# PSUM as four pairs of banks, and the second tiles' masks after their scores, in a planned fp32 transformer kernel

## The chip, the core and the metric

The kernel runs on one NeuronCore of a Trainium2 chip. The metric is device time in microseconds (us) of one execution, the median of several. The engines are called by the names of the profile: PE (matmuls; PEld is its weight load), ACT, DVE and POOL (elementwise work), SP (which issues the DMAs).

## What is computed

The input is 32 sequences of 256 tokens and 128 channels. Each goes through half a feed-forward block, an attention over channels, and half a feed-forward block again, always with a residual; the two blocks use the same weights. A feed-forward block (`_L0_ffn_ref`) has two layers, and each layer is a local attention followed by a gated MLP:

```
qkv = shift_token(x) @ wqkv              # 8 heads of 64
q, k = l2norm(q) * qs, l2norm(k) * ksc   # then rotary
sim = q . k over a window                # key j of query i: i-64 <= j <= i
x = x + (softmax(sim) @ v) @ wo
h = layernorm(shift_token(x)) @ w1 + b1  # 128 -> 2 x 341
x = x + (a * gelu(g)) @ w2 + b2
```

So there are 32 x 2 x 2 = 128 layers to compute, each in two tiles of 128 tokens. All data is fp32.

## The kernel before

**A plan in place of loops.** The Python code first makes a list of operations (`plan.op`), each with its engine, a cost in us, the operations that it follows, and the places that it uses: SBUF and PSUM buffers, taken by kind with `plan.take`. `Plan.order` then sets the order of all engines. It goes through the list in stretches of 15 PE operations, tries 16 orders for the next 60 PE operations with its own costs, keeps the one in which PE ends first, and commits the stretch. `Plan.go` takes the operation that can start first by `begin`, gives it its buffers (the free buffer of its kind that came free first) and moves the clock of its engine. `Plan.run` then writes the instructions in that order, with scheduling otherwise off. The waits between engines are put in afterwards by the framework, which looks at the tiles that instructions read and write.

**PSUM.** There are eight banks of 512 fp32 for each partition. Lines 112 and 113 make two "wide" tiles of two banks and four "bank" tiles of one bank, each a tile of its own. A wide tile holds the Q/K projection of a token tile (`project`, L197), the scores (`scores`, L247 and L255) and the attention output (`attended`, L289). A bank holds the V projection (L231), sets of transposes (`transposed`, L140), the output projection (L312), one third of the MLP's first product (L381), its second product (L414), and the products of the channel attention (L458). ACT empties most banks by copies (L130, `evac`; DVE in a few cases); DVE and ACT read the wide tiles (L203, L205, L208, L261, L264, L296, L297).

**Scores.** For each token tile, keys are cut into frames of 96 for blocks of 32 queries. Two bf16 matmuls of an identity with the mask (128x128 weights, 384 columns: four head pairs by 96) first write the mask into both banks, with start set; then 32 matmuls on 64x32 parts of the array add the scores. A value product is 32 matmuls of 96 rows by 32 columns (`attended`). An fp32 product is two matmul records in the profile, a transpose or a bf16 product one.

**Other buffers.** "gg" (three) holds the gelu half of the MLP between ACT (L389) and DVE (L396); "ob" (two) holds the divided attention output between DVE (L297) and its transposes. The prediction numbers lines as in the kernel before, except where it quotes the changed program.

Of the kernel before, what the change touches and what calls it, by code (L numbers as in the profile page):

```python
# [8 lines left out]
F32 = mybir.dt.float32  # L9
# [6 lines left out]
P = 128  # L16
# [24 lines left out]
def kernel(ctx: ExitStack, tc: tile.TileContext, ins: dict, out: bass.AP):  # L41
# [39 lines left out]
    for kind, n, shape in (  # L81
        ("x", CHAINS + 2, [P, NT, P]),
        ("y", CHAINS, [P, NT, P]),
        ("y3", CHAINS - 1, [P, NT, 3, P // 2]),
        ("xT", 2, [P, NT, P]),
        ("hT", SETS + 2, [P, SEQ]),
        ("qT", 4, [P, PAIRS, P]),
        ("kT", SETS, [P, PAIRS, SEQ]),
        ("vt", 2 * SETS + 1, [P, HEADS, DH + 1]),
        ("vm0", 3, [FR, 1, HEADS, DH + 1]),  # L90
        ("vm1", 2, [FR, 3, HEADS, DH + 1]),
        ("sq", 3, [P, 2, HEADS, DH]),
        ("qk", 4, [P, 2, HEADS, DH]),
        ("pr", 3, [P, 2, PAIRS, FR]),
        ("pT", 4, [P, PAIRS, P]),
        ("ob", 2, [P, INNER]),
        ("oT", 2, [P, PAIRS, P]),
        ("uT", 2, [P, len(HCH), SEQ]),
        ("z", 3, [P, NT, P]),
        ("zT", 2, [P, NT, P]),  # L100
        ("gg", 3, [P, SEQ]),
        ("cp", CHAINS + 1, [P, P]),
        ("ssq", 4, [P, 2, HEADS]),
        ("rn", 4, [P, 2, HEADS]),
        ("mx", 4, [P, 2, PAIRS]),
        ("rd", 4, [P, 2, PAIRS, 1]),
        ("st", 4, [P, NT, nc.vector.BN_STATS_DIM]),
        ("mv", 4, [P, NT, nc.vector.BN_AGGR_DIM]),
        ("v1", 12, [P, NT]),
    ):  # L110
        plan.places(kind, [hold.tile(shape, F32, name=f"{kind}{i}") for i in range(n)])
    for kind, n, shape in (("wide", 2, [P, 2, 512]), ("bank", 4, [P, 512])):
        plan.places(kind, [psum.tile(shape, F32, tag=f"{kind}{i}", name=f"ps_{kind}{i}", bufs=1) for i in range(n)])
    plan.places("sequence", range(CHAINS))

    for t in plan.free["vt"]:
# [122 lines left out]
    def scores(qT, kT, t, after):  # L239


        wide, mx, pr = (plan.take(k) for k in ("wide", "mx", "pr"))
        s = lambda: wide.t[:, :, : PAIRS * FR].rearrange("p r (j k) -> p r j k", k=FR)

        def mm(e):
            for r in range(2):
                nc.tensor.matmul(  # L247
                    s()[:, r], identh, masks[t].unsqueeze(1).to_broadcast([P, PAIRS, FR]), start=True, stop=False
                )
            for j in range(PAIRS):  # L250
                for b in range(NB):
                    k0 = frame(t, b)
                    for r in range(2):
                        row = slice(r * DH, (r + 1) * DH)
                        nc.tensor.matmul(  # L255
                            s()[b * BLK : (b + 1) * BLK, r, j, :], qT.t[row, j, b * BLK : (b + 1) * BLK],
                            kT.t[row, j, k0 : k0 + FR], start=False, stop=j == PAIRS - 1,
                        )

        m = plan.op("PE", 1.35, mm, after + [made["masks"][t]], [wide, qT, kT, mx, pr])  # L260
        a = plan.op("DVE", 0.87, lambda e: nc.vector.tensor_reduce(mx.t, s(), AX.X, ALU.max), [m], [wide, mx])  # L261
        b = plan.op(
            "DVE", 0.87,
            lambda e: nc.vector.tensor_sub(pr.t, s(), mx.t.unsqueeze(3).to_broadcast([P, 2, PAIRS, FR])),  # L264
            [a], [wide, mx, pr],
        )
        c = plan.op("ACT", 0.75, lambda e: nc.scalar.activation(pr.t, pr.t, AF.Exp), [b], [pr], table="exp")  # L267
        return pr, c

    def attended(pr, vt, vm, ob, t, after, values):  # L270

        mo, rd = plan.take("wide"), plan.take("rd")
        pTs, copies = [plan.take("pT") for r in range(2)], []
        for r in range(2):
            _, b = transposed(
                lambda r=r: [pr.t[:, r, j, :] for j in range(PAIRS)], PAIRS, lambda r=r: pTs[r].t[:FR], pTs[r],
                after, [pr, ob] + pTs, FR,
            )
            copies.append(b)
# [12 lines left out]

        m = plan.op("PE", 1.05, mm, copies + values, [mo, vt, vm, rd, ob] + pTs)

        def div(e):
            nc.vector.reciprocal(rd.t, o()[:, :, :, DH : DH + 1])  # L296
            nc.vector.tensor_mul(  # L297
                ob.t.rearrange("p (j r d) -> p r j d", r=2, d=DH), o()[:, :, :, 0:DH],
                rd.t.to_broadcast([P, 2, PAIRS, DH]),
            )  # L300

        return plan.op("DVE", 0.84, div, [m], [mo, rd, ob])
# [345 lines left out]
class Plan:  # L648
# [5 lines left out]

    SYNC = {"PE": 0.16, "DVE": 0.08, "ACT": 0.08, "POOL": 0.09, "SP": 0.08}
    TAIL = {"PE": 0.165, "ACT": 0.105, "DVE": 0.085, "POOL": 0.04, "SP": 0.0}
    RATHER = 1.0
    TABLE = 1.3
    TURNS = ("wide", "bank")
# [10 lines left out]
        pass  # L670

    def __init__(self):
        self.free, self.ops, self.rank, self.base = {}, [], 0, 0

    def places(self, kind, tiles):
        self.free[kind] = list(tiles)
# [1 line left out]
    def take(self, kind):  # L678
        return Plan.Place(kind)

    def op(self, engines, us, fn, after, uses, late=0.0, table=None, apart=False):
        o = Plan.Op()
        o.engines = (engines,) if isinstance(engines, str) else engines
        o.us = us if isinstance(us, tuple) else (us,)
        o.fn, o.late, o.table, o.apart = fn, late, table, apart
        o.rank, o.step = self.rank, len(self.ops) - self.base
        o.uses, o.then = [], []
        o.after = list(after)
        for d in o.after:
            d.then.append(o)  # L690
        self.ops.append(o)
        self.use(o, uses)
        return o
# [14 lines left out]
    def order(self, together):  # L708
# [2 lines left out]
        import random  # L711

        self.clock = dict.fromkeys(("PE", "DVE", "ACT", "POOL", "SP"), 0.0)
        self.table, self.through = None, 0
        self.room = {k: list(v) for k, v in self.free.items()}
        self.since = {k: [0.0] * len(v) for k, v in self.room.items()}
        for o in self.ops:
# [25 lines left out]

    def save(self):
        copy = lambda d: {k: list(v) for k, v in d.items()}
        return dict(self.clock), self.table, copy(self.room), copy(self.since), list(self.ready), len(self.out), self.through

    def back(self, saved):

        clock, self.table, room, since, ready, n, self.through = saved  # L750
        self.clock, self.ready = dict(clock), list(ready)
        self.room, self.since = ({k: list(v) for k, v in d.items()} for d in (room, since))
        for thing, state in reversed(self.undo):
            thing.__dict__.update(state)
        self.undo = []
        del self.out[n:]

    def lacks(self, o):
# [4 lines left out]
                need[p.kind] = need.get(p.kind, 0) + 1  # L763
        return need

    def begin(self, o, engine):

        t = max(o.given[engine], self.clock[engine], self.clock["POOL"] if o.apart else 0.0)
        sync = self.SYNC[engine]
        for p in o.uses:  # L770
            if p.last and p.last[1] != engine and p.kind in self.TURNS:
                t = max(t, p.last[0] + sync)
        for k, n in self.lacks(o).items():
            if len(self.room[k]) < n:
                return None
            t = max(t, (min(self.since[k]) if n == 1 else sorted(self.since[k])[n - 1]) + sync)
        return t

    def choose(self, o):

# [12 lines left out]
    def go(self, until, later, chance):  # L793
# [16 lines left out]
        while heap and (until is None or self.through < until):  # L810
            first, _, o = heapq.heappop(heap)
            choice = self.choose(o)
            if choice is None:
                barred.setdefault(next(k for k, n in self.lacks(o).items() if len(self.room[k]) < n), []).append(o)
                continue

            engine, t, us, rank = choice
# [4 lines left out]
            for p in o.uses:  # L822
                self.undo.append((p, dict(p.__dict__)))
                if p.t is None:
                    i = min(range(len(self.room[p.kind])), key=lambda i: self.since[p.kind][i])
                    p.t = self.room[p.kind].pop(i)
                    self.since[p.kind].pop(i)
                    taken.append((p, p.t))
                    for d in barred.pop(p.kind, []):
                        enter(d)  # L830
# [1 line left out]
            self.clock[engine] = t + us  # L832
            if o.apart:
                self.clock["POOL"] = t + us
            self.through += engine == "PE"
            self.undo.append((o, {"done": None}))
            o.done = (t + us + o.late + self.TAIL[engine], engine)
            if engine == "ACT" and o.table not in (None, self.table):
# [5 lines left out]
            for p in o.uses:  # L844
                p.left -= 1
                p.end, p.last = max(p.end, o.done[0]), o.done
                if not p.left:
                    self.room[p.kind].append(p.t)
                    self.since[p.kind].append(p.end)
                    for d in barred.pop(p.kind, []):  # L850
                        enter(d)
            for d in o.then:
                self.undo.append((d, {"wait": d.wait}))
# [57 lines left out]
```

## Time and profile before

| what | value |
|---|---|
| median of 3 runs | 2841.89 us (2840.95 to 2842.41) |
| the profiled execution | 2842.17 us |
| its span, first to last instruction | 2840.1 us |
| mean granted PE clock | 0.997 |
| busy: PE, DVE, ACT, POOL | 2788.2, 2135.1, 1993.7, 2302.2 us |
| DMA | 129.82 MB, mean 46 GB/s |

The page gives for each engine its busy time, then its busy share in 40 slices of the span (a digit is tenths). Groups of instructions are named by line, engine, output and inputs, with count and mean duration. A line of waits reads: who waited, for whom, us in total, how many times, the longest. A line of the timeline reads: start in us, length, engine, line, operation, output and inputs, rows by columns of the array, shape, count; a row merges equal neighbours, and since matmuls are pipelined its length overlaps the next start.

### The profile page before, as it was taken

How to read it: one execution, taken by the hardware profiler on the slowest of the kernel's cores; microseconds unless marked ns; L12 is line 12 of the kernel's file. 1: busy time of each engine (PE TensorE's matmuls, PEld its weight loads, DVE VectorE, ACT ScalarE, POOL GpSimd, SP SyncE). 2: the span in 40 equal slices, each digit the busy share in tenths (PEclk: the TensorE clock that was granted, in tenths of full speed). 3: DMA queues.
4: the chain of work that ended last, by engine and by line, in shares of the span. 5: the costliest groups of instructions: out<-in, count | busy, mean ns of one | idle time of the engine just before them, and what ended most of it. 6: DMA issues, size and time to landing. Idle time of an engine off the chain costs nothing.

```text
span 2840.1 us, 106723 instructions
## 1 busy us (share of the span) xinstructions
PE 2788.2 (98%) x46200; PEld 2114.4 (74%) x46200; DVE 2135.1 (75%) x3764; ACT 1993.7 (70%) x3601; POOL 2302.2 (81%) x2098
## 2 busy tenths in 40 slices
PE   7999999999999999999999999999999999999999
PEld 4777777777777777777777777777777777777677
DVE  5778778778777778677777777877787777777776
ACT  4776776767677776767777776776767677776675
POOL 8988879698889778787798878878788788875975
PEclk9999999999999999999999999999999999999999
DMA  3111121111211111111112112111121111110211
GB/s 109 31 46 44 38 52 47 39 51 37 55 38 47 46 40 48 38 49 45 44 51 53 46 36 52 46 36 47 47 55 47 37 46 44 43 46 20 53 42 41
DMA packets 125726, 129.82 MB, mean 46 GB/s; under 512 B 56606, under 2 KB 75592, under 8 KB 125256
## 3 DMA queue, kind: packets, MB, share of 16 engines
q1 hardware_dynamic: 124440, 122.60, 16.5%
q8 instruction: 363, 5.95, 0.9%
q14 instruction: 107, 0.88, 0.1%
q10 hardware_dynamic: 816, 0.39, 0.0%
HBM read 8.13 MB, written 4.19 MB: 4 GB/s over the span
## 4 chain that ended last, share of the span: by engine, by line
PE 86%; DVE 6%; ACT 3%; POOL 3%; issue 1%; DMA 1%; SPq 0%; ACTq 0%; DVEq 0%; POOLq 0%
PE ps_bank L140 20%; PE ps_wide L197 14%; PE ps_bank L381 11%; PE ps_wide L289 9%; PE ps_bank L312 8%; PE ps_wide L255 7%; PE ps_bank L231 7%; PE ps_bank L414 6%; PE ps_wide L247 3%; PE ps_bank L458 1%; PE ps_bank L178 1%; DVE qk L205 1%; DVE sq L208 1%; ACT sq L203 1%; POOL rn L124 1%
## 5 line engine op out<-in xcount | busy, mean ns | idle before, releaser
L124 POOL TENSOR_TENSOR rn<-ssq,mhalf 128x16 f32<-128x16 f32 x256 | 748.3, 2923 | 21.3
L222 POOL TENSOR_TENSOR qk<-qk,sq 128x1024 f32<-128x1024 f32 x256 | 606.4, 2370 | 163.8 <-DVE sq L208 83.4
L225 POOL TENSOR_TENSOR qk<-qk,rn 128x1024 f32<-128x1024 f32 x256 | 487.7, 1908 | 10.4
L197 PE MATMUL ps_wide<-wqkv,hT 128*128 128x512 f32 x1024 | 489.2, 600 | 2.0 <-ACT hT L130 1.2
L205 DVE TENSOR_TENSOR qk<-ps_wide,tab 128x1024 f32<-128x1024 f32 x256 | 312.2, 1219 | 184.7 <-ACT sq L203 101.7
L381 PE MATMUL ps_bank<-zT,w 128*128 128x256 f32 (+1 forms) x1536 | 379.3, 383 | 2.8 <-DVE zT L130 1.7
L203 ACT ACTIVATE sq<-ps_wide 128x1024 f32<-128x1024 f32 x256 | 262.5, 1025 | 154.2 <-PE ps_wide L197 91.6
L208 DVE TENSOR_TENSOR sq<-ps_wide,tab 128x1024 f32<-128x1024 f32 x256 | 311.4, 1217 | 66.8 <-ACT sq L203 32.6
L130 ACT COPY pT<-ps_bank 96x512 f32<-96x512 f32 x505 | 283.3, 584 | 101.1 <-PE ps_bank L140 98.7
L214 DVE TENSOR_REDUCE ssq<-sq 128x16 f32<-128x1024 f32 x256 | 310.0, 1211 | 57.2 <-ACT sq L203 56.4
L381 PEld LDWEIGHTS ps_bank<-zT,w 128*128 128x128 f32 (+1 forms) x1536 | 257.8, 178 | 70.8 <-issue 15.0
L140 PE MATMUL ps_bank<-ident,pr 128*96 128x128 f32 x2048 | 290.2, 275 | 5.1 <-ACT pr L267 2.4
L140 PE MATMUL ps_bank<-ident,qk 128*128 128x128 f32 x2048 | 290.8, 276 | 3.1 <-POOL qk L225 2.4
L261 DVE TENSOR_REDUCE mx<-ps_wide 128x8 f32<-128x768 f32 x256 | 242.9, 949 | 62.8 <-PE ps_wide L255 61.7
L197 PEld LDWEIGHTS ps_wide<-wqkv,hT 128*128 128x128 f32 x1024 | 179.4, 191 | 145.7 <-issue 133.3
L289 PE MATMUL ps_wide<-vt,pT 96*32 96x65 f32 x8192 | 282.1, 221 | 3.5 <-ACT pT L130 1.4
L289 PE MATMUL ps_wide<-vm,pT 96*32 96x65 f32 x8192 | 283.9, 221 | 1.5 <-DVE sq L208 0.7
L312 PE MATMUL ps_bank<-wo,oT 128*128 128x128 f32 x2048 | 275.9, 279 | 2.7 <-ACT oT L130 1.0
L140 PEld LDWEIGHTS ps_bank<-ident,qk 128*128 128x128 f32 x2048 | 236.4, 141 | 48.1 <-issue 24.0
L312 PEld LDWEIGHTS ps_bank<-wo,oT 128*128 128x128 f32 x2048 | 251.2, 191 | 27.1 <-issue 10.3
L140 PEld LDWEIGHTS ps_bank<-ident,pr 128*96 128x96 f32 x2048 | 225.1, 126 | 60.7 <-issue 29.3
L289 PEld LDWEIGHTS ps_wide<-vt,pT 96*32 96x32 f32 x8192 | 240.6, 109 | 37.8 <-issue 17.6
(101 smaller groups left out, 5430.1 us busy)
## 6 DMA issues: line engine op xcount, KB each, us to landing
vm<-vt SPq DMA_DIRECT2D x256, 195.0 KB
vm<-vt SPq DMA_DIRECT2D x256, 130.0 KB
vm<-vt SPq DMA_DIRECT2D x256, 65.0 KB
y<-y SPq DMA_DIRECT2D x128, 56.0 KB
x<-in_x SPq DMA_DIRECT2D x32, 128.0 KB
out<-x SPq DMA_DIRECT2D x32, 128.0 KB
y<-y SPq DMA_DIRECT2D x128, 7.5 KB
y<-y SPq DMA_DIRECT2D x128, 0.2 KB
```

The lines of the kernel that those rows point to most:

```text
L124: nc.gpsimd.tensor_tensor(dst, src, mhalf[:, :n], ALU.pow)
L140: nc.tensor.transpose(pt.t[:rows, j * P : (j + 1) * P], src, ident)
L197: nc.tensor.matmul(wide.t[:, a], lhsT(), wqkv[:, l, a * INNER : (a + 1) * INNER], start=True, stop=True)
L203: "ACT", 0.92, lambda e: nc.scalar.activation(sq.t, pq(), AF.Square), [m], [wide, sq]
L205: c = plan.op("DVE", 1.14, lambda e: nc.vector.tensor_mul(qk.t, pq(), cos), [m] + made["tables"][l], [wide, qk])
L208: lambda e: nc.vector.tensor_mul(sn.t.rearrange(five, x=2), pq().rearrange(five, x=2)[:, :, :, ::-1, :], sin.rearrange(five, x=2)),
L214: "DVE", 1.13, lambda e: nc.vector.tensor_reduce(ssq.t, sq.t, AX.X, ALU.add), [s], [sq, ssq]
L222: f = plan.op("POOL", 2.42, lambda e: nc.gpsimd.tensor_add(qk.t, qk.t, sn.t), [c, i], [qk, sn])
L225: lambda e: nc.gpsimd.tensor_mul(qk.t, qk.t, rn.t.unsqueeze(3).to_broadcast([P, 2, HEADS, DH])),
L289: nc.tensor.matmul(o()[q, r, j, :], pTs[r].t[:FR, j, q], v[:, 2 * j + r, :], start=True, stop=True)
L312: nc.tensor.matmul(pw.t[:, :P], oT.t[:, j, :], wo[:, l, j, :], start=j == 0, stop=j == PAIRS - 1)
L381: nc.tensor.matmul(pa.t[:w, i * SEQ : (i + 1) * SEQ], w1[:, l, i * HID + c0 : i * HID + c0 + w], zf(), start=True, stop=True,)
```

## The change

PSUM becomes four tiles of two banks each. A wide place takes a whole pair that is free in both banks; a bank place takes one bank, that is, a slice `[:, h, :]` of a pair's tile. Among the banks free in time it takes one of a pair whose other bank is not free, if there is one. What is given back may serve either kind.

For the second token tile of a layer (t = 1) the mask goes last: the first score matmul of each part has start set, and the mask is added after all scores. The mask is zero in the middle third of each frame of that tile, and only its first and last thirds are now loaded and added: 4 x 2 x 32 columns in place of 4 x 96. For the first tile all stays.

Each PE operation carries a form: how it finds and leaves the array (whole, parts, values). The plan keeps the form last left; a table of costs for changes of form stands beside it, which no line reads. The cost of the second tiles' scores in the plan goes from 1.35 to 1.16. There is one more place of "ob" and of "gg".

```diff
-        ("ob", 2, [P, INNER]),
+        ("ob", 3, [P, INNER]),
-        ("gg", 3, [P, SEQ]),
+        ("gg", 4, [P, SEQ]),
-    for kind, n, shape in (("wide", 2, [P, 2, 512]), ("bank", 4, [P, 512])):
-        plan.places(kind, [psum.tile(shape, F32, tag=f"{kind}{i}", name=f"ps_{kind}{i}", bufs=1) for i in range(n)])
+    plan.pairs = [psum.tile([P, 2, 512], F32, tag=f"pair{i}", name=f"ps_{i}", bufs=1) for i in range(4)]
+    plan.places("bank", [(i, h) for i in range(4) for h in range(2)])
...
         def mm(e):
-            for r in range(2):
-                nc.tensor.matmul(
-                    s()[:, r], identh, masks[t].unsqueeze(1).to_broadcast([P, PAIRS, FR]), start=True, stop=False
-                )
+            thirds = masks[t].rearrange("p (c k) -> p c k", k=BLK)[:, :: 1 + t, :]
+            def mask():
+                for r in range(2):
+                    nc.tensor.matmul(
+                        s()[:, r].rearrange("p j (c k) -> p j c k", k=BLK)[:, :, :: 1 + t, :], identh,
+                        thirds.unsqueeze(1).to_broadcast([P, PAIRS, thirds.shape[1], BLK]), start=t == 0, stop=t == 1,
+                    )
+            if t == 0:
+                mask()
...
-                            kT.t[row, j, k0 : k0 + FR], start=False, stop=j == PAIRS - 1,
+                            kT.t[row, j, k0 : k0 + FR], start=t == 1 and j == 0, stop=t == 0 and j == PAIRS - 1,
+            if t == 1:
+                mask()
-        m = plan.op("PE", 1.35, mm, after + [made["masks"][t]], [wide, qT, kT, mx, pr])
+        m = plan.op(
+            "PE", (1.35, 1.16)[t], mm, after + [made["masks"][t]], [wide, qT, kT, mx, pr],
+            form=(("all", "parts"), ("parts", "all"))[t],
+        )
...
+    CHANGE = {("all", "parts"): 0.09, ("all", "values"): 0.09, ("values", "values"): -0.11}
...
+    def whole(self):
+        since = {}
+        for (i, _), t in zip(self.room["bank"], self.since["bank"]):
+            since.setdefault(i, []).append(t)
+        return [(max(ts), i) for i, ts in since.items() if len(ts) == 2]
...
+    def grab(self, p, t):
+        room, since = self.room, self.since
+        if p.kind == "wide":
+            i = min(self.whole())[1]
...
+            p.t, p.bank = self.pairs[i], i
+            return
+        pick = lambda n: since[p.kind][n]
+        if p.kind == "bank":
+            here = [i for i, _ in room["bank"]]
+            pick = lambda n: (max(since["bank"][n] + self.SYNC["PE"], t), here.count(here[n]), since["bank"][n])
+        n = min(range(len(room[p.kind])), key=pick)
+        p.t = p.bank = room[p.kind].pop(n)
+        since[p.kind].pop(n)
+        if p.kind == "bank":
+            p.t = self.pairs[p.bank[0]][:, p.bank[1], :]
...
+    def give(self, p):
...
+        self.room["bank"] += [(p.bank, 0), (p.bank, 1)] if p.kind == "wide" else [p.bank]
+        self.since["bank"] += [p.end] * (2 if p.kind == "wide" else 1)
+        return "wide", "bank"
...
-            self.through += engine == "PE"
+            if engine == "PE":
+                self.through, self.array = self.through + 1, o.form[1]
```

More of the change, by code (lines that the diff above doesn't have):

```diff
@@ L291, in mm @@
                         )
-        m = plan.op("PE", 1.05, mm, copies + values, [mo, vt, vm, rd, ob] + pTs)
+        m = plan.op("PE", 1.05, mm, copies + values, [mo, vt, vm, rd, ob] + pTs, form=("values", "values"))
         def div(e):
@@ L672, in __init__ @@
     def __init__(self):
-        self.free, self.ops, self.rank, self.base = {}, [], 0, 0
+        self.free, self.ops, self.rank, self.base, self.pairs = {}, [], 0, 0, []
     def places(self, kind, tiles):
@@ L679, in take, with op @@
         return Plan.Place(kind)
-    def op(self, engines, us, fn, after, uses, late=0.0, table=None, apart=False):
+    def op(self, engines, us, fn, after, uses, late=0.0, table=None, apart=False, form=("all", "all")):
         o = Plan.Op()
@@ L684, in op @@
         o.us = us if isinstance(us, tuple) else (us,)
-        o.fn, o.late, o.table, o.apart = fn, late, table, apart
+        o.fn, o.late, o.table, o.apart, o.form = fn, late, table, apart, form
         o.rank, o.step = self.rank, len(self.ops) - self.base
@@ L713, in order @@
         self.clock = dict.fromkeys(("PE", "DVE", "ACT", "POOL", "SP"), 0.0)
-        self.table, self.through = None, 0
+        self.table, self.array, self.through = None, "all", 0
         self.room = {k: list(v) for k, v in self.free.items()}
@@ L745, in save @@
         copy = lambda d: {k: list(v) for k, v in d.items()}
-        return dict(self.clock), self.table, copy(self.room), copy(self.since), list(self.ready), len(self.out), self.through
+        return dict(self.clock), (self.table, self.array), copy(self.room), copy(self.since), list(self.ready), len(self.out), self.through
     def back(self, saved):
-        clock, self.table, room, since, ready, n, self.through = saved
+        clock, (self.table, self.array), room, since, ready, n, self.through = saved
         self.clock, self.ready = dict(clock), list(ready)
@@ L773, in begin @@
         for k, n in self.lacks(o).items():
+            if k == "wide":
+                whole = self.whole()
+                if not whole:
+                    return None
+                t = max(t, min(whole)[0] + sync)
+                continue
             if len(self.room[k]) < n:
@@ L777, in begin @@
         return t
+    def grab(self, p, t):
+        room, since = self.room, self.since
+        if p.kind == "wide":
+            i = min(self.whole())[1]
+            for h in range(2):
+                n = room["bank"].index((i, h))
+                room["bank"].pop(n), since["bank"].pop(n)
+            p.t, p.bank = self.pairs[i], i
[10 more added lines that the diff above has]
+    def give(self, p):
+        if p.kind not in ("wide", "bank"):
+            self.room[p.kind].append(p.t)
+            self.since[p.kind].append(p.end)
+            return (p.kind,)
+        self.room["bank"] += [(p.bank, 0), (p.bank, 1)] if p.kind == "wide" else [p.bank]
+        self.since["bank"] += [p.end] * (2 if p.kind == "wide" else 1)
+        return "wide", "bank"
     def choose(self, o):
@@ L813, in go @@
             if choice is None:
-                barred.setdefault(next(k for k, n in self.lacks(o).items() if len(self.room[k]) < n), []).append(o)
+                lacks = self.lacks(o).items()
+                kind = next((k for k, n in lacks if k != "wide" and len(self.room[k]) < n), "wide")
+                barred.setdefault(kind, []).append(o)
                 continue
@@ L824, in go @@
                 if p.t is None:
-                    i = min(range(len(self.room[p.kind])), key=lambda i: self.since[p.kind][i])
-                    p.t = self.room[p.kind].pop(i)
-                    self.since[p.kind].pop(i)
+                    self.grab(p, t)
                     taken.append((p, p.t))
@@ L847, in go @@
                 if not p.left:
-                    self.room[p.kind].append(p.t)
-                    self.since[p.kind].append(p.end)
-                    for d in barred.pop(p.kind, []):
+                    for d in [d for k in self.give(p) for d in barred.pop(k, [])]:
                         enter(d)
```

## The prediction

> **What bounds the kernel now.** I read the page's busy times and slices first, then the groups and waits of TensorE (PE), then its timeline, and last the built programs.
>
> ```profile
> span 2840.1 us, 106723 instructions
> PE 2788.2 (98%) x46200; PEld 2114.4 (74%) x46200; DVE 2135.1 (75%) x3764; ACT 1993.7 (70%) x3601; POOL 2302.2 (81%) x2098
> ...
> PE   7999999999999999999999999999999999999999
> ...
> PEclk9999999999999999999999999999999999999999
> ```
>
> PE is busy 98% of the span in every slice but the first, at a granted clock of 0.997. But matmul records overlap, so 98% does not say that PE never waits. The distance between starts does:
>
> ```profile
> 1504.63 0.49 PE L247 MATMUL ps_wide<-mask,identh 128*128 128x384 bf16 x2
> 1505.05 1.00 PE L255 MATMUL ps_wide<-kT,qT 64*32 64x96 f32 x64
> 1505.98 1.60 PE L414 MATMUL ps_bank<-w,uT 128*128 128x128 f32 x12
> 1507.42 2.75 PE L381 MATMUL ps_bank<-zT,w 128*128 128x256 f32 x12
> 1510.01 0.60 PE L140 MATMUL ps_bank<-ident,pr 128*96 128x128 f32 x4
> 1510.45 0.49 PE L247 MATMUL ps_wide<-mask,identh 128*128 128x384 bf16 x2
> ```
>
> One step of the plan costs PE the time to the next start: masks 0.42 us, scores 0.93, four transposes 0.44. I took for each of the 21 kinds of PE step its back-to-back distance (the fastest twentieth) and multiplied by its count: 256 Q/K projections at 1.716, 384 first MLP products at 0.863, 256 value products at 1.046, 256 output products at 0.891, 1,280 transposes of four at 0.436, 256 V projections at 0.858, 256 scores at 1.345, 128 second MLP products at 1.337, and 125 us of small ones: **2684.9 us**. What starts exceed this by is 141.7 us: 236 entries from a whole-array step into a value product at 0.092 (21.7); **65.6** in 640 short bubbles, mostly 0.042, 0.056 or 0.104, after which no release had just come; and **54.4** in waits that ended just before the start: 20.1 for a PSUM bank still being read, 34.3 for data. With 13.6 for the start and the end: 2684.9 + 21.7 + 65.6 + 54.4 + 13.6 = 2840.2. The profiled execution took 2842.17, 2.1 more than its span, and 0.3 more than the median of 2841.89.
>
> ```profile
> PE ps_bank L178 <- ACT y L163: 14.9, 3, 9.6
> PE ps_bank L458 <- DVE cp L487: 3.0, 5, 1.1
> PE ps_bank L140 <- POOL qk L225: 2.4, 4, 0.9
> PE ps_bank L140 <- ACT pr L267: 2.4, 3, 1.7
> ```
>
> These are PE's longest waits: one at the start, the rest under 2 us each. The step order, which the planner fixes, hides nearly all of the other engines' work behind PE. That is what the change can gain little on and lose much of.
>
> **The change, part by part.**
>
> *Masks.* The 128 second tiles load 256 mask columns per bank in place of 384. Two mask matmuls start 0.163 apart for 384 columns, so one of 256 takes 0.109: 256 x 0.054 = **-13.9 us**, all on PE. The new write skips 32 of every 96 columns; no row of before has a stepped write. Bounds: -13.9, and, were a stepped write to take twice as long (0.218), +14.1. I take -13.9: the nearest row, this mask itself, reads and writes runs of 96 at one column per 0.42 ns, and 32-column runs are the only difference. The Trainium skill, "PSUM — Partial Sum Buffer", Specifications, speaks against it: it says that a non-contiguous pattern slows matmuls significantly. By that the term would go towards the upper bound.
>
> *Order of masks and scores.* From masks to scores PE loses 0.092 (0.418 less two times 0.163); in ten places of before where a mask follows scores it loses 0.003, and where a value product follows scores (14) 0.001. So only the entry into small tiles costs. The entry moves ahead of the second tile's scores and is saved where small tiles already ran. Counting neighbours in the two built orders: 256 entries to masks-then-scores and 236 to values before; 128, 105 and 204 after, and 21 from a last mask into values: 492 against 458, **-3.1 us**. Value products that follow each other go from 6 to 22; such a pair takes 1.958, not 2 x 1.046: 16 x 0.134 = **-2.1**. Entering scores from values (16 places) is unseen: 0 to 0.092 each, at most 1.5, left out.
>
> *Costs in the plan.* The table of switch costs is written but never read; only the smaller figure for a second tile's scores acts. It changes the order, priced with that.
>
> *More places, gg and ob.* These can only remove waits for data, 34.3 us together, of which about 13 lie in the first 200 us. Nil to -20; I take nil.
>
> *PSUM as four pairs.* Now any pair can be two single banks. The gain is at most the 20.1 us of bank waits. The cost isn't in the diff but in the built program. A pair is one tile, and a bank a slice of it. I followed each wait's count to the instruction that raises it. Before, all 3,339 waits of ACT and DVE for PE name the step that filled the bank they read. After, **1,178 of 2,512** name a later one, always one that fills the pair's other bank: 872 on ACT, 306 on DVE. A reader of bank 0 waits until PE is through with bank 1, and PE's next write to either waits for readers of both: of the releases that PE waits for, 565 read only the other bank. PE also fills one pair in two consecutive steps 1,163 times (33 before), for the planner prefers to break a pair already broken. The planner knows nothing of this. An example, the first V projections in PE's order and then ACT's:
>
> ```
> L232 Matmult ps_218<-wqkv,hT_115 128x512 x2
> L131 TensorCopy vt_129<-ps_218 128x8x64 [waits PE_49]
> L131 TensorCopy vt_130<-ps_218 128x8x64
> ```
>
> The first copy waits for both matmuls; the second has nothing left to wait for.
>
> What each costs: a reader is late by the PE steps between, 0.44 us at the median on ACT (a set of transposes) and 0.86 on DVE (one product), in sum 772 and 501 us. Queued behind it are its engine's copies, squares and exponentials, for which PE waits in turn. ACT's idle time is 846 us and DVE's 705, so much hides. What lands on PE I tallied at each PE step: from the last PE step that its releaser depends on, along the chain of readers, their durations from before's rows, for instance
>
> ```profile
> L130 ACT COPY pT<-ps_bank x505: 560/582/634, 45.0 to 2811.5; 96x512 f32<-96x512 f32 x169
> L130 ACT COPY oT<-ps_bank x253: 560/586/645, 52.1 to 2817.1; 128x512 f32<-128x512 f32 x127
> L389 ACT ACTIVATE gg<-ps_bank,b x384: 452/473/496, 78.0 to 2833.2; 128x256 f32<-128x256 f32 x121, 85x256 f32<-85x256 f32 x71
> L396 DVE SCALAR_TENSOR_TENSOR uT<-ps_bank,b,gg x384: 447/475/485, 79.7 to 2833.7; 128x256 f32<-128x256 f32 x127, 85x256 f32<-85x256 f32 x65
> ```
>
> plus 0.2 from PE's end to a reader's start and 0.06 back (both the shortest in before); less the PE steps that stand in between. Where PE's next step needs what the step just ahead filled, nothing stands in between and it pays 0.2 + 0.58 + 0.06 = 0.84 us. In before this charges 60 us at 149 steps, where 54.4 was measured. In after it charges **281 us at 570 steps**. It counts some stalls twice, as one stall gives time for the next chain; taking out what was charged inside the same stretch leaves 39 before (15 too few) and 215 after. So 281 x 54/60 = 253 one way, 215 + 15 = 230 the other. I take **235**, 181 more than now. Low end 117: only the last reader's own duration. High end 215 x 54/39 = 298, or more if lateness piles up. The Trainium skill, the same page, its summary of rules, says to guard PSUM by bank; the program guards by pair, so by that rule the cost would be nil.
>
> **Sum.** 2842.2 - 13.9 - 3.1 - 2.1 + 181 = **3004 us**. ACT's function loads fall from 178 to 154 (1.28 us each), but ACT isn't on the path by itself.
>
> **Rivals.**
> *A, faster.* The pairs do what they are for: bank waits go (20), the pair waits hide in the idle time of ACT and DVE: 2842.2 - 19 - 20 = 2803. For it: 30% of ACT is idle. Against it: in 77 places the next PE step needs a reader of the one just filled, where nothing can hide it. It decides if all waits stay under 73 us together. 6%.
> *B, mildly slower.* Only the reader's own time lands: 2842.2 - 19 - 54 + 117 = 2886. 12%.
> *C, much slower.* Lateness piles up in the queues of ACT and DVE. Mine lets 181 of their 1,273 us of lateness reach PE; at three tenths, 382: 2842.2 - 19 + 382 = 3205. For it: ACT's 1,994 busy and 772 late come to 2,766 of 2,840. Against it: a slower PE gives ACT more room. 14%.
> *No change*, everything cancelling: 2%.
> The forecast, 2900 to 3100: 66%.
>
> Range 2875 to 3120: it leaves out A, no change, a third of B and over half of C, 2 in 10. A measurement of this kernel can tell 0.2% from no change. Faster 6%, same 2%, slower 92%.
>
> **What would show it.** PE's busy share falls, its waits by line are no longer led by the start but by transposes and products behind ACT copies, hundreds of them, of 0.2 to 0.9 us. ACT's idle time before copies grows. Mask matmuls of the second tile start 0.109 apart if the stepped write is free. Wrong would be a PE as dense as now, or mask matmuls at 0.2.

## The result, and the profile after

The changed kernel takes **3016.16 us** (median of five, 3013.52 to 3017.97) where the kernel before took 2842.41 beside it: 1.0608 times as long, with a 95% interval of 1.0597 to 1.062. The forecast was 3004. The profiled execution took 3013.52 us, 1.8 more than its span, at a mean granted clock of 0.999. From here on a line number belongs to the kernel named with it; in the changed kernel `evac` is L131, `transposed` L141, the output projection L326 and its addition by DVE L331.

The head of the page of the changed kernel, with PE's slices and its clock:

```profile
span 3011.7 us, 106559 instructions
PE 2825.6 (94%) x46200; PEld 2111.1 (70%) x46200; DVE 2148.8 (71%) x3775; ACT 1954.6 (65%) x3566; POOL 2300.9 (76%) x2098
...
PE   7999999999999999999999999999999999998998
PEclk9999999999999999999999999999999999999999
```

PE falls from 98% to 94%, at the same clock. The other engines do as much as before, in a longer span. The slices show two digits under 9 behind the first. They hide the loss: 6% of each slice is too little for a digit, and each matmul's record reaches over the start of the next.

PE's waits, of the changed kernel (who waited, for whom; us in total, times, longest):

```profile
PE ps L179 <- ACT y L164: 9.9, 2, 9.6
PE ps L141 <- ACT qT L131: 7.8, 14, 1.6
PE ps L141 <- ACT pT L131: 6.2, 11, 1.2
PE ps L141 <- ACT gg L403: 6.2, 10, 1.8
PE ps L141 <- DVE uT L410: 6.1, 9, 0.9
```

No pair dominates. Behind the start come transposes (L141) that wait for whatever ACT or DVE reads: Q copies, probabilities, gelus, products. The telling lines are those of the readers. Groups by line and form, with the idle time just before them and what ended it; first the copies of K transposes and the output additions of the kernel before:

```profile
L130 ACT COPY kT<-ps_bank 128x512 f32<-128x512 f32 x254 | 149.2, 592 | 36.2 <-PE ps_bank L140 35.0
L317 DVE TENSOR_TENSOR y<-ps_bank,y 128x128 f32<-128x128 f32 x256 | 71.7, 284 | 65.3 <-PE ps_bank L312 59.2 <-ACT kT L130 3.3 <-ACT vt L130 1.3
```

and the same groups of the changed kernel:

```profile
L131 ACT COPY kT<-ps 128x512 f32<-128x512 f32 x253 | 149.1, 591 | 74.5 <-PE ps L141 36.3 <-PE ps L326 8.8 <-DVE y L331 8.1
L331 DVE TENSOR_TENSOR y<-ps,y 128x128 f32<-128x128 f32 x256 | 72.3, 287 | 137.5 <-PE ps L141 27.3 <-PE ps L326 25.7 <-PE ps L395 12.7
```

A K copy needs its transposes and nothing else. Before, 35.0 of its 36.2 us of idle time ended with them. Now 36.3 of 74.5 do; the rest ends with output products (L326), DVE's additions and others that have no data for it. The additions idle 137.5 us in place of 65.3, and their own products (L326) end only 25.7 of it; transposes end more. These are the pair's other bank, seen from outside.

One such place in the timeline of the changed kernel, engine by engine (start, us, then in brackets the idle time before and what ended it). PE:

```profile
1145.86 0.60 PE L141 MATMUL ps<-ident,qk 128*128 128x128 f32 x4
1146.30 1.06 PE L326 MATMUL ps<-wo,oT 128*128 128x128 f32 x8
1147.19 1.88 PE L198 MATMUL ps<-wqkv,hT 128*128 128x512 f32 x4
1149.82 0.66 PE L141 MATMUL ps<-ident,qk 128*128 128x128 f32 x4 [0.74 <-ACT gg L403]
```

ACT:

```profile
1147.39 0.58 ACT L131 COPY qT<-ps 128x512 f32<-128x512 f32 x1 [1.61 <-PE ps L326]
1147.99 1.28 ACT L403 ACT_TABLE_LOAD   x1
1149.29 0.47 ACT L403 ACTIVATE gg<-ps,b 128x256 f32<-128x256 f32 x1
1149.66 1.02 ACT L204 ACTIVATE sq<-ps 128x1024 f32<-128x1024 f32 x1
```

DVE:

```profile
1148.01 0.29 DVE L331 TENSOR_TENSOR y<-ps,y 128x128 f32<-128x128 f32 x1 [1.55 <-ACT qT L131]
1150.58 0.48 DVE L410 SCALAR_TENSOR_TENSOR uT<-ps,b,gg 128x256 f32<-128x256 f32 x1 [2.28 <-PE ps L141]
```

The Q transposes end at about 1146.46 and fill bank 1 of a pair. Their copy does not start there. PE goes on with an output product into bank 0 of the same pair, and the copy starts only when that is through, at 1147.39. DVE's addition, which reads that product in bank 0, then waits for ACT's copy out of bank 1. ACT, late by now, loads its function table and makes a gelu from bank 0 of another pair. PE's next transposes go into bank 1 of that pair and wait for the gelu: PE stands for 0.74 us. And DVE's L410, which reads bank 0, waits for those transposes into bank 1. Some of this idle time is a wait for data: the Q transposes end at 1146.46, the product at 1147.36, the gelu at 1149.76. But none of the four waits ends with data, or with the bank that the waiting instruction itself uses.

**The account.** For all kernels I took PE's start-to-start distances as the prediction did, with one set of back-to-back distances and entries, which moves the prediction's sums of before by up to 2.2 us (2704.4 where it had 2684.9 and 21.7). The excess is sorted by what came just before the start: a release by a reader of only the pair's other bank, a release of the same bank, or data, each less than 0.075 us ahead ("waits"); a release 0.075 to 0.25 ahead ("just before"); none (bubbles). With some 15 us for start and end a row sums to the span. One of the eleven executions of change_own_tiles_2_4 took 7012 us, for a reason that was not found; it moves that median by less than 0.1 us.

| kernel | median | back to back, with entries | waits: other bank | same bank | data | just before | bubbles |
|---|---|---|---|---|---|---|---|
| before | 2842.41 | 2704.4 | 0 | 20.3 | 34.2 | 7.4 | 58.9 |
| changed | 3016.16 | 2685.2 | 72.0 | 60.6 | 60.5 | 40.8 | 76.9 |
| halves_same_order | 3159.87 | 2704.4 | 228.1 | 31.0 | 42.3 | 47.1 | 89.6 |
| pairs_alone | 3053.11 | 2701.5 | 66.9 | 57.8 | 89.1 | 32.3 | 86.0 |
| change_spread_banks | 3128.59 | 2684.1 | 219.0 | 20.2 | 41.7 | 54.8 | 93.8 |
| masks_same_order | 2830.82 | 2689.9 | 0 | 21.9 | 37.3 | 8.0 | 57.5 |
| places_alone | 2830.55 | 2702.9 | 0 | 21.5 | 25.8 | 8.1 | 54.2 |
| change_own_tiles_2_4 | 2838.93 | 2689.3 | 0 | 24.6 | 43.4 | 12.5 | 51.4 |
| own_banks_2_4 | 2825.99 | 2689.3 | 0 | 19.1 | 43.9 | 7.4 | 50.7 |
| change_same_order_own_banks | **2786.19** | 2685.2 | 0 | 9.2 | 21.7 | 6.6 | 50.6 |
| own_banks_fewer_places | 2803.42 | 2684.1 | 0 | 12.5 | 29.8 | 5.8 | 53.9 |
| own_banks_other_seed | 2808.14 | 2683.1 | 0 | 5.7 | 38.9 | 7.7 | 57.5 |
| own_banks_table_read | 2814.07 | 2682.2 | 0 | 7.8 | 44.3 | 6.5 | 57.0 |

From before to changed, PE's own work falls by 19.2 us and the excess rises by 189.9: waits by 138.6 (to 193.1 us in 406 places, 0.40 at the median), "just before" by 33.4, bubbles by 18. Of the 138.6, 72.0 are waits for the other bank itself. The rest are waits for data and for the same bank, whose readers are late; in the same order without shared tiles (change_same_order_own_banks) these two are 21.7 and 9.2.

### The profile page after: what moved, and what is told of

It reads as the page before. It is cut to its first block, busy times and chain, and to the rows that moved or that the text cites. A ratio compares the mean times of both kernels' runs of the same rounds, so it can differ in the third digit from the quotient of the medians.

```text
span 3011.7 us, 106559 instructions
## 1 busy us (share of the span) xinstructions
PE 2825.6 (94%) x46200; PEld 2111.1 (70%) x46200; DVE 2148.8 (71%) x3775; ACT 1954.6 (65%) x3566; POOL 2300.9 (76%) x2098
## 5 line engine op out<-in xcount | busy, mean ns | idle before, releaser
L198 PE MATMUL ps<-wqkv,hT 128*128 128x512 f32 x1024 | 491.5, 603 | 4.8 <-ACT hT L131 3.7
L206 DVE TENSOR_TENSOR qk<-ps,tab 128x1024 f32<-128x1024 f32 x256 | 312.0, 1219 | 150.2 <-ACT sq L204 96.5
L395 PE MATMUL ps<-zT,w 128*128 128x256 f32 (+1 forms) x1536 | 381.7, 384 | 19.5 <-DVE uT L410 4.7
L204 ACT ACTIVATE sq<-ps 128x1024 f32<-128x1024 f32 x256 | 262.4, 1025 | 151.1 <-PE ps L198 105.9
L131 ACT COPY pT<-ps 96x512 f32<-96x512 f32 x499 | 280.4, 585 | 123.2 <-PE ps L141 60.9
L209 DVE TENSOR_TENSOR sq<-ps,tab 128x1024 f32<-128x1024 f32 x256 | 311.2, 1215 | 44.3 <-ACT sq L204 23.0
L141 PE MATMUL ps<-ident,qk 128*128 128x128 f32 x2048 | 292.3, 276 | 25.7 <-DVE uT L410 3.4
L141 PE MATMUL ps<-ident,pr 128*96 128x128 f32 x2048 | 288.7, 275 | 21.9 <-ACT pr L281 3.9
L410 DVE SCALAR_TENSOR_TENSOR uT<-ps,b,gg 128x256 f32<-128x256 f32 (+1 forms) x384 | 175.3, 478 | 173.5 <-ACT gg L403 120.4
L326 PE MATMUL ps<-wo,oT 128*128 128x128 f32 x2048 | 278.1, 280 | 17.3 <-ACT oT L131 5.2
L141 PEld LDWEIGHTS ps<-ident,qk 128*128 128x128 f32 x2048 | 234.5, 141 | 84.6 <-issue 45.9
L326 PEld LDWEIGHTS ps<-wo,oT 128*128 128x128 f32 x2048 | 251.6, 192 | 57.8 <-ACT oT L131 16.4
L303 PE MATMUL ps<-vm,pT 96*32 96x65 f32 x8192 | 282.3, 221 | 4.8 <-DVE pr L278 1.3
L303 PE MATMUL ps<-vt,pT 96*32 96x65 f32 x8192 | 280.4, 221 | 4.9 <-issue 2.0
L141 PEld LDWEIGHTS ps<-ident,pr 128*96 128x96 f32 x2048 | 224.7, 126 | 80.9 <-issue 27.2
```

Source lines behind the costliest of these rows:

```text
L131: lambda e: (nc.scalar.copy if e == "ACT" else nc.vector.tensor_copy)(dst(), src()), after, uses,
L141: nc.tensor.transpose(pt.t[:rows, j * P : (j + 1) * P], src, ident)
L198: nc.tensor.matmul(wide.t[:, a], lhsT(), wqkv[:, l, a * INNER : (a + 1) * INNER], start=True, stop=True)
L206: c = plan.op("DVE", 1.14, lambda e: nc.vector.tensor_mul(qk.t, pq(), cos), [m] + made["tables"][l], [wide, qk])
L209: lambda e: nc.vector.tensor_mul(sn.t.rearrange(five, x=2), pq().rearrange(five, x=2)[:, :, :, ::-1, :], sin.rearrange(five, x=2)),
L303: nc.tensor.matmul(o()[q, r, j, :], pTs[r].t[:FR, j, q], v[:, 2 * j + r, :], start=True, stop=True)
```

## The experiments

**My theory**: the cost is the tile, not the plan. The framework orders the users of a tile, so two banks in one tile tie PE, ACT and DVE to each other; the rest of the change gains. **Rivals**: the planner's new order or its free pool of banks costs the time; or the stepped, later masks do.

**1. halves_same_order.** The kernel before, with its four single banks made halves of two tiles. PE, ACT, DVE and POOL have the same instructions in the same order; only waits differ.

```diff
-    for kind, n, shape in (("wide", 2, [P, 2, 512]), ("bank", 4, [P, 512])):
...
+    halves = [psum.tile([P, 2, 512], F32, tag=f"half{i}", name=f"ps_half{i}", bufs=1) for i in range(2)]
+    plan.places("bank", [halves[i][:, h, :] for i in range(2) for h in range(2)])
```

> The kernel before with one thing changed: its four single banks are slices of two two-bank tiles. The plan can't see it, so every engine's order of instructions is that of before; only the waits that follow from shared tiles are new. Theory 1 (the loss of the change is readers and writers of one bank waiting for users of the other bank of its tile): much slower than before; the tally of the prediction, made for this program, charges 328 us at 666 PE steps, scaled to what before and after measured 374, so about 3150 us (3080 to 3250). Theory 2 (the loss comes from the order that the pooled pairs lead the plan to, not from waits): no change, 2842 us.

Measured: 3159.87 us, 1.1116 times before (1.1101 to 1.1132). The head of its page and its longest PE waits:

```profile
span 3158.3 us, 106546 instructions
...
PE 2901.2 (92%) x46200; PEld 2109.7 (67%) x46200; DVE 2148.6 (68%) x3764; ACT 2013.2 (64%) x3601; POOL 2301.1 (73%) x2098
```

```profile
PE ps_half L141 <- ACT pT L131: 22.2, 44, 1.3
PE ps_half L141 <- DVE uT L397: 15.4, 24, 1.6
PE ps_half L141 <- ACT vt L131: 12.1, 25, 0.9
```

PE's work is that of before to the tenth (2704.4 in the table), and 317 us beyond it are added, 228.1 of them in waits for the other bank. With no line of the work or the order changed, tile sharing alone costs this.

**2. masks_same_order.** The kernel before with the second tiles' masks last and cut; the plan keeps its cost of 1.35, so the order stays.

```diff
+            thirds = masks[t].rearrange("p (c k) -> p c k", k=BLK)[:, :: 1 + t, :]
...
+                        thirds.unsqueeze(1).to_broadcast([P, PAIRS, thirds.shape[1], BLK]), start=t == 0, stop=t == 1,
```

> The kernel before with the second tiles' masks after their scores and cut to two thirds of the columns, at the plan cost of before, so that the order stays that of before; PSUM, gg and ob as before. Theory 1 and the prediction's mask term: 128 x 0.109 us less for columns and some 0.6 us less for entries, so about 2828 us (2823 to 2833). Theory 3 (the stepped PSUM write or the late mask costs time and is part of the loss): 2842 us or more, and mask matmuls more than 0.109 us apart.

Measured: 2830.82 us, 0.9957 (0.9945 to 0.997). A second tile in its PE timeline:

```profile
1516.50 1.00 PE L263 MATMUL ps_wide<-kT,qT 64*32 64x96 f32 x64
1517.43 0.39 PE L251 MATMUL ps_wide<-mask,identh 128*128 128x256 bf16 x2
1517.66 0.60 PE L140 MATMUL ps_bank<-ident,pr 128*96 128x128 f32 x4
```

From the masks' start to the next step are 0.23 us for two, against 0.42 from the masks to the scores, entry included, in the prediction's excerpt. In the changed kernel the two starts are 0.119 apart and the last mask is 0.109 ahead of the next whole-array step. The mask edit gains, and takes no part in the loss.

**3. change_own_tiles_2_4.** The changed kernel with the PSUM of before: two tiles of two banks, four of one. All other parts stay, and the planner makes a new order.

```diff
-    plan.pairs = [psum.tile([P, 2, 512], F32, tag=f"pair{i}", name=f"ps_{i}", bufs=1) for i in range(4)]
-    plan.places("bank", [(i, h) for i in range(4) for h in range(2)])
+    for kind, n, shape in (("wide", 2, [P, 2, 512]), ("bank", 4, [P, 512])):
```

> The changed kernel with PSUM as before: two tiles of two banks and four of one, each its own tile; masks, plan costs, gg and ob as changed. Theory 1: the false waits are gone, and with them nearly the whole loss: 2830 to 2860 us, around before. Theory 2: also near before, since the pooling is gone too. Theory 3: 2900 or more, since masks, costs and places are all still there.

Measured: 2838.93 us, 0.9985 (0.9976 to 0.9995). The loss is gone. The gain is less than runs 2 and 10 give singly, since this order waits more for data (43.4 against 34.2). Run 9 shows how much an order may move.

**4. change_same_order_own_banks.** The changed kernel's plan and its order untouched, but each bank is a tile of its own and a pair is two tiles. What reads a whole pair is cut in two, one for each bank: 256 more ACT and 1,536 more DVE instructions.

```diff
-    plan.pairs = [psum.tile([P, 2, 512], F32, tag=f"pair{i}", name=f"ps_{i}", bufs=1) for i in range(4)]
+    plan.pairs = [
+        [psum.tile([P, 512], F32, tag=f"pair{i}{h}", name=f"ps_{i}{h}", bufs=1) for h in range(2)] for i in range(4)
+    ]
...
-            "ACT", 0.92, lambda e: nc.scalar.activation(sq.t, pq(), AF.Square), [m], [wide, sq]
+            "ACT", 0.92, lambda e: [nc.scalar.activation(sq.t[:, a], pq(a), AF.Square) for a in range(2)], [m], [wide, sq]
...
-            p.t = self.pairs[p.bank[0]][:, p.bank[1], :]
+            p.t = self.pairs[p.bank[0]][p.bank[1]]
```

> The changed kernel with its plan, PE's order included, untouched, but each of the eight banks a tile of its own. A pair is two such tiles, so each ACT or DVE instruction that read a whole pair is now two of half the size: 256 more on ACT, 1,536 more on DVE, at the plan's old costs. Theory 1: the 1,178 false waits and the 565 of PE go; 2800 to 2850 us, below before unless the smaller instructions cost more than their waits gave. Theory 2: the order is the culprit and is the same, so 3000 us or more, the more so for the added instructions.

Measured: 2786.19 us (2784.58 to 2789.9), 0.9804 (0.9791 to 0.9818): faster than the kernel before by 56 us and than the changed kernel by 230, and below the range that was expected. From its page, and its longest PE waits:

```profile
span 2788.1 us, 108885 instructions
...
PE 2746.8 (99%) x46200; PEld 2111.2 (76%) x46200; DVE 2210.5 (79%) x5311; ACT 1980.6 (71%) x3822; POOL 2299.9 (82%) x2098
```

```profile
PE ps L181 <- ACT y L166: 11.5, 2, 9.5
PE ps L266 <- issue: 3.9, 6, 0.9
PE ps L234 <- ACT hT L133: 2.2, 3, 0.9
```

and the two groups of readers from above:

```profile
L133 ACT COPY kT<-ps 128x512 f32<-128x512 f32 x253 | 149.5, 594 | 45.4 <-PE ps L143 44.6
L338 DVE TENSOR_TENSOR y<-ps,y 128x128 f32<-128x128 f32 x256 | 72.4, 286 | 82.1 <-PE ps L333 73.6 <-PE ps L143 4.4 <-PE ps L490 0.9
```

The same work in the same order: the K copies again wait for their own transposes (44.6 of 45.4), the additions for their own products (73.6 of 82.1). Outside the pairs of instructions that pass data or read the same bank, DVE's waits for ACT sum to 5.3 us before, 123.0 in the changed kernel and 12.1 here, ACT's for DVE to 5.0, 120.8 and 15.4. The halved readers cost 62 us more of DVE and 26 of ACT (2148.8 to 2210.5, 1954.6 to 1980.6), hidden behind PE. The order that the rival blames is that of the fastest kernel of the study.

**5. pairs_alone.** The kernel before with the four pooled pairs only: no masks, no forms, no new places.

```diff
+    plan.pairs = [psum.tile([P, 2, 512], F32, tag=f"pair{i}", name=f"ps_{i}", bufs=1) for i in range(4)]
+    plan.places("bank", [(i, h) for i in range(4) for h in range(2)])
...
+            p.t = self.pairs[p.bank[0]][:, p.bank[1], :]
```

> The kernel before with only PSUM as four pairs, pooled as in the change; masks, plan costs, gg and ob as before. Theory 1: the whole loss is here, with 17 to 19 us of masks and entries missing and an order of its own; the tally charges 226 us here against 216 for the change, so about 3040 us (3000 to 3090). Theory 2 says the same. If the masks, the lower plan cost or the extra places were behind the loss, this would stay near 2842.

Measured: 3053.11 us, 1.0744 (1.0727 to 1.076). This one part makes the whole loss; the others, with the order that they bring, take 37 us off it.

**6. change_spread_banks.** The changed kernel, but a single bank is taken from a pair whose other bank is free, if there is one.

```diff
-            pick = lambda n: (max(since["bank"][n] + self.SYNC["PE"], t), here.count(here[n]), since["bank"][n])
+            pick = lambda n: (max(since["bank"][n] + self.SYNC["PE"], t), -here.count(here[n]), since["bank"][n])
```

> The changed kernel with one sign turned: among the banks free in time, a bank place takes one of a pair whose other bank is free too. Theory 1: neighbours share pairs less at once but a broken pair stays broken longer, and every pair is broken; the tally charges 282 us at 638 steps against 216 at 463, so about 3085 us (3040 to 3150), slower than the change. Theory 2 (the preference for broken pairs makes the bad order): faster than the change, under 2980.

Measured: 3128.59 us, 1.1005 (1.099 to 1.102), 112 us over the changed kernel. The waits for the other bank rise from 72.0 to 219.0. So the preference for a pair already broken, which the prediction held against the change, is not what loses the time. That it saves 112 us isn't shown: the planner also makes another order here, and how much of the 112 is the order isn't separated.

**7. own_banks_2_4.** Own banks and halved readers, but two fixed pairs and four fixed single banks, so in the order of run 3.

```diff
+    banks = [psum.tile([P, 512], F32, tag=f"bank{i}", name=f"ps_{i}", bufs=1) for i in range(8)]
+    plan.places("wide", [banks[0:2], banks[2:4]])
+    plan.places("bank", banks[4:])
```

> As change_same_order_own_banks (each bank a tile of its own, pair readers cut in two), but with the places of before: two fixed pairs and four single banks; the order is that of change_own_tiles_2_4. It tells the freedom of the pool from the cutting of the readers. Theory 1a (the gain over change_own_tiles_2_4 comes from the freedom of the pool): 2830 to 2845 us, like that run. Theory 1b (it comes from readers cut in two, which release the first bank earlier): about 2790.

Measured: 2825.99 us, 0.9944 (0.9931 to 0.9956). Neither expectation holds alone. Against run 3, in the same order, cutting the wide tiles and their readers gains 13 us. Run 4, which also chooses its banks freely, is 40 us faster than this run: bank waits of 9.2 in place of 19.1, data waits of 21.7 in place of 43.9. Its order is another one, and how much of the 40 is the order isn't separated (run 9).

**8. own_banks_fewer_places.** Run 4 with three places of gg and two of ob.

```diff
-        ("ob", 3, [P, INNER]),
+        ("ob", 2, [P, INNER]),
...
-        ("gg", 4, [P, SEQ]),
+        ("gg", 3, [P, SEQ]),
```

> As change_same_order_own_banks with gg and ob as before (three and two places). If the one more place of each is worth something: slower by up to 10 us, 2790 to 2796. The prediction took it at nil: 2783 to 2790.

Measured: 2803.42 us, 0.9861 (0.9848 to 0.9875), 17 over run 4 and over both ranges expected. The order is another one, so the 17 us can't be put down to the places (run 9).

**9. own_banks_other_seed.** Run 4, with another seed for the planner's random orders.

```diff
-        at, chance, kept = 0, random.Random(1), {}
+        at, chance, kept = 0, random.Random(2), {}
```

> change_same_order_own_banks with another seed for the orders that the plan tries, nothing else. It shows how far the time moves with the order alone. If orders found with this plan and these places are worth about the same, 2780 to 2800; then differences of 10 us between kernels of different order tell nothing, and 45 us do.

Measured: 2808.14 us, 0.9881 (0.9868 to 0.9895), 22 over run 4 and over the range expected. One other seed moves the time by as much as run 8 does. Differences of about 20 us between kernels with different orders can't be put down to an edit; those of runs 1, 2 and 4, with orders kept, can.

**10. places_alone.** The kernel before with the places of gg and ob only.

```diff
-        ("ob", 2, [P, INNER]),
+        ("ob", 3, [P, INNER]),
...
-        ("gg", 3, [P, SEQ]),
+        ("gg", 4, [P, SEQ]),
```

> The kernel before with one more place each of gg and ob, nothing else. The prediction took this at nil and bounded it at 20 us less: 2822 to 2842. The tally charges 33 us against 39 before, so 2834 or so. If the 17 us between own_banks_fewer_places and change_same_order_own_banks are the places' worth whatever PSUM is like: about 2825.

Measured: 2830.55 us, 0.9964 (0.995 to 0.9978). Data waits fall from 34.2 to 25.8. That is the direction that was expected of places, but the order is another one too.

**11. own_banks_table_read.** Run 4 with the table of switch costs read by the plan.

```diff
-            "PE", (1.35, 1.16)[t], mm, after + [made["masks"][t]], [wide, qT, kT, mx, pr],
+            "PE", (1.345, 1.145)[t], mm, after + [made["masks"][t]], [wide, qT, kT, mx, pr],
...
+            us += self.CHANGE.get((self.array, o.form[0]), 0.0) if engine == "PE" else 0.0
```

> change_same_order_own_banks with the plan's table of switch costs in use: begin and end of each PE step are charged by the form that the array was left in. Fewer entries into small parts (3 us by the counts of neighbours), and steps timed closer to the measured ones: 2775 to 2795, if the order found has no worse waits. If the unread table were behind the loss of the change, it would show here as a large gain, 2700 or so.

Measured: 2814.07 us, 0.9901 (0.9888 to 0.9915), 28 over run 4 and over the range expected. PE's work falls by 3.0 us (2685.2 to 2682.2), as the switches saved account for, and data waits rise from 21.7 to 44.3. By run 9 that may be the order's luck. Whether the table pays stays open.

## Why the prediction was right

- *What bounds the kernel.* Right. PE's starts, not its busy share, carried the account: the changed kernel is 94% busy, and 310.7 us of its 3011.7 lie beyond back-to-back work.
- *Masks (-13.9) and order of masks and scores (-3.1).* Right in sum, slightly off in size. The stepped write takes 0.119 us for 256 columns where 0.109 was taken, so two masks cost 0.228 and not 0.218, 1.3 us in all. Back-to-back work and entries together changed by -19.2 us; the prediction's three terms come to -19.1. That the sum fits is partly luck. In seven places of the changed kernel scores follow scores, which never happens before; where PE doesn't wait there, they start 0.737 apart and not 0.926. That saves 1.3 us, which no term had, and makes up for the masks. It also goes against the reading that only the entry into small tiles costs. The Trainium skill, "PSUM — Partial Sum Buffer", Specifications, which spoke for the upper end, is not borne out for this write: two masks that skip 32 of every 96 columns cost 0.010 us more than the 0.218 of unskipped ones. Whether the skipping makes the 0.010 isn't shown.
- *Entering scores from values* was left out at 0 to 1.5 us. It costs 0.003 in each of 16 places.
- *gg and ob (nil, at most -20).* Not settled. Run 10 gives -12 and run 8 -17, but run 9 moves 22 by the order alone. Neither bears out the choice of nil, nor rules it out.
- *The pair as one tile (+181).* Right in mechanism, shown by runs 1 and 4, which change the tiles and keep the order. In size, the excess rose by 189.9. It divides differently. Waits in the prediction's sense come to 193.1 us where it took 235, 42 too many, at 406 steps where the tally charged 570. What it called bubbles and held at 65.6 (here bubbles and "just before" together) went from 66.3 to 117.7, 51 more: a PE that comes late also collects short distances that no release marks, which no term had. That these two errors, 42 and 51 us, nearly cancel is luck. They leave 9 of the 12 us by which the forecast was short; the rest is the profiled execution, 2.6 under the median. One mechanism was not in its lateness of 772 and 501 us, which counts waits for PE alone: ACT and DVE also wait for each other's reads of the two banks (123.0 and 120.8 us, 5.3 and 5.0 before).
- *"PE also fills one pair in two consecutive steps".* True, but as a reproach not borne out: run 6, with the preference turned round, takes 112 us more, in an order of its own.
- *Rival A (2803)* failed, as its own condition says: 193 us of waits where 73 was the limit. What it hoped for is real all the same: without shared tiles, run 4 reaches 2786. *Rival C* (3205) failed too: it needed 382 us of the counted lateness to reach PE, and the excess rose by 189.9. Runs 1 and 6 come near it with 3160 and 3129, but whether lateness piles up there was not counted. *Rival B* failed, as more than the last reader's own duration lands on PE.
- *What would show it.* PE's share fell, ACT's idle time grew (846 to 1057 us), and the waits are hundreds of short ones, spread over transposes behind ACT and DVE. The start still leads the list of waits with 9.9 us, since no single pair exceeds it; it was said that it wouldn't.

## What to carry to other kernels

Where a framework derives waits from tiles, a tile is the unit of waiting: as here, two independent PSUM banks in one tile make the engines that use either wait for each other, and a planner that counts free banks won't see it. Give each bank a tile of its own and cut the readers of a pair in two; here that turned a loss of 174 us into a gain of 56, with the same order of work. Before believing an edit that also reshuffles a planned order, run the plan with another seed: here that alone was worth 22 us.

## What the runs showed of the hardware

- A change of array form costs PE time. Entering small parts from whole-array work costs 0.092 to 0.094 us, into a value product or a first tile's scores. On the way out it makes hardly a difference which other form follows: scores take 0.926 us to the next start before whole-array work, 0.927 before values and 0.929 before a mask; values take 1.046 before whole-array work and 1.048 before scores. It is less where the same form goes on: 0.737 from scores to scores, 0.934 from values to values. So the distances taken as back to back hold 0.19 and 0.11 us that are there only when the form changes. The Trainium skill, "TensorEngine Tiling (Array Packing)", Key Properties, says that each change of tiling mode drains TensorE; these distances agree with it, though no run shows the drain itself. Two sets of scores in a row in the changed kernel, where PE takes 1.66 us from the first set's start to the mask:

```profile
133.04 1.73 PE L264 MATMUL ps<-kT,qT 64*32 64x96 f32 x128
134.70 0.39 PE L252 MATMUL ps<-mask,identh 128*128 128x256 bf16 x2
```

- Halving a PSUM read costs little per instruction: ACT's square took 1025 ns for 128x1024 and 599 for 128x512, DVE's product with the table 1219 and 683, its reduction 949 and 550. Two halves take 12 to 17% longer than the whole.
- Bubbles of mostly 0.042, 0.056 or 0.104 us, with no release just before, are in every run, from 50.6 us (run 4) to 93.8 (run 6), and tend to be more where PE waits more. What makes them was not found.
